# A graph layer and a routed FFN on one core: phase 3 begins with the pair of blocks that phase 2 ends with, two FFN chunks go ahead, batch norms take a power on GpSimd

## The chip, the core and the metric

The kernel runs on one core of one Trainium2 chip, as one launch. The time is device microseconds (us) of the whole launch: the median of three runs is 2086.63 us (2084.45, 2086.63 and 2086.96).

A core has five engines that run side by side, each its own list of instructions in order: TensorE (PE in the profile, matrix products and transposes), VectorE (DVE), ScalarE (ACT), GpSimd (POOL) and SyncE (SP, which here only starts DMAs). They wait for each other by semaphores. SBUF is the on-chip memory of 128 partitions, PSUM the banks that matrix products write, HBM the memory outside. A scheduler orders the instructions of each engine from the order of the program text and estimated costs; `tc.keep_in_program_order` pins one.

## What is computed

```python
def ref(x, src, dst, edge_attr):            # x 10000 x 512, 5000 edges with 64 attributes
    xn = layernorm(x)
    msg = relu(xn[src] + edge_attr @ W_e + b_e)
    h = (1 + eps) * xn + segment_sum(msg, dst)
    h = silu(bn(h @ W1 + b1, g1, beta1))     # 512 -> 1024, bn: batch norm over all 10000 rows
    h = silu(bn(h @ W2 + b2, g2, beta2))     # 1024 -> 512
    x = x + h
    g = layernorm(x) in groups of 16 rows    # routed FFN: 16 experts in 4 sets
    perm = (logits == max over the 16 rows of a group),  logits = g @ controller + tie
    inner = relu(sum over rows of (g @ f1) * perm)
    return x + sum over expert, set of (inner @ f2) * perm
```

All is in float32. Both batch norms need the mean and variance of each feature over all 10000 rows, so nothing behind one can begin before the last row ahead of it is done.

## The kernel before

**Phase 1** gathers the 5000 source rows of x (40 tiles of 128, `xgs`), makes the messages and adds them into `agg` in HBM by indirect DMAs of GpSimd, each group of four after the one before.

**Phase 2** (loop L354-376) goes over ten pairs of blocks of 500 rows. A `Block` loads x and agg rows (`load`, L309-314, tiles `xt` and `at`), norms and adds them, and turns them feature-major into `hb`. `block_sums` (L110) makes five sums of quarters of `hb`, s1, s3 and s6 on GpSimd and s4 and s7 on VectorE; `strassen` (L125) makes the product with W1 from seven quarter products (named 1 to 7; in a profile by their PSUM banks w, v, y, z, x and so on) instead of eight. For each pair m runs over 4 slices of the output. The result h1 (two feature halves x two blocks x 500) gets its batch statistics by `bn_stats` and is stored to `h1s` in HBM.

**`batchnorm`** (L75) makes scale and shift of each feature: `bn_aggr` for each block of 128 features, then the root on ScalarE (`AF.Sqrt`), a reciprocal and three short operations on VectorE.

**Phase 3** (L379-400) makes the sums of W2's quarters (`weight_sums`, five VectorE instructions), and then for each of ten pairs loads `hb` (4 MB) from `h1s` in one DMA, applies batch norm and Silu in place on ScalarE (L388, 16 instructions), makes five block sums (L122, whole: kb is 4, so an instruction covers 4 x 500 or, where the profile shows 128x2000, all four slices) and runs `strassen` for m = 0 and 1. Only for the first pair the products come in the order `FIRST`, 2, 5, 4, 3, 1, 6, 7. The result goes to `h2s` in HBM in two stores a pair. `hb` has two buffers.

**The FFN** (L735 on) goes over 20 chunks of 512 rows (the last has 272). `load_y` reads four tiles `yt` of the chunk from `h2s`, `load_x` two tiles `x2` of x, `silu` applies batch norm 2 and Silu, `residual` transposes and adds, `norm` is the layer norm on GpSimd (its root as `ALU.pow` with the tile `power`), `flip` and `logits` and `choose` make the routing, `gather`, `inner`, `relu`, `outer`, `turn`, `split` and `scatter` the FFN. `step(a, b, d, e, nxt)` (L662-733) works on four chunks at once: a gets its residual, norm and routing, b its gather and first product, d its second product, e its way back; for `nxt`, the chunk after a, loads and Silu are issued.

```python
    chunks[0].load_y()
    chunks[0].load_x()
    chunks[0].silu()
    nc.sync.dma_start(out=f1_sb, in_=a["L0_ffn_f1"].rearrange("(k p) n -> p k n", p=P))
    ...
    for c in range(NC + 3):
        step(at(c), at(c - 1), at(c - 2), at(c - 3), at(c + 1))
```

The weights f1 (one DMA) and f2 (eight) are issued behind chunk 0's loads, on the same queue as all loads and stores (SP). The tiles `yt` have one buffer for each k, so a chunk's load waits for the residual of the chunk before.

Of the kernel before, what the change touches and what calls it, by code (L numbers as in the profile page):

```python
# [8 lines left out]
F32 = mybir.dt.float32  # L9
# [41 lines left out]
def gnn_ffn_kernel(ctx: ExitStack, tc: tile.TileContext, a: dict, out: bass.AP):  # L51
# [7 lines left out]
    h1s = tc.dram_tile([NP, P, MH, 2, TB], F32, name="h1s")  # L59
# [7 lines left out]
    power = const.tile([P, KH, 1], F32, name="power")  # L67
# [7 lines left out]
    def batchnorm(name, stats, blocks, g, beta):  # L75

        mv = const.tile([P, blocks, 2], F32, name=name + "_mv")
        sc = const.tile([P, blocks], F32, name=name + "_sc")
        sh = const.tile([P, blocks], F32, name=name + "_sh")
        for m in range(blocks):  # L80
            nc.vector.bn_aggr(out=mv[:, m, :], in_=stats[:, m, :, :].rearrange("p c s -> p (c s)"))
        nc.scalar.activation(sc, mv[:, :, 1], AF.Sqrt, bias=eps_t, scale=1.0)
        nc.vector.reciprocal(sc, sc)
        nc.vector.tensor_mul(sc, sc, g)
        nc.vector.tensor_mul(sh, mv[:, :, 0], sc)
        nc.vector.tensor_sub(sh, beta, sh)
        return sc, sh
# [22 lines left out]
    def block_sums(pool, name, hb, kb):  # L110

        def q(i, j):
            return hb[:, i * kb:(i + 1) * kb, j, :]

        r = {2: q(0, 0), 5: q(1, 1)}
        for n, eng, x0, x1, op in ((3, nc.gpsimd, q(0, 1), q(1, 1), ALU.subtract),
                                   (1, nc.gpsimd, q(0, 0), q(1, 1), ALU.add),
                                   (4, nc.vector, q(1, 0), q(0, 0), ALU.subtract),
                                   (6, nc.gpsimd, q(0, 0), q(0, 1), ALU.add),
                                   (7, nc.vector, q(1, 0), q(1, 1), ALU.add)):  # L120
            r[n] = pool.tile([P, kb, TB], F32, name=f"{name}_s{n}", bufs=1)
            eng.tensor_tensor(r[n], x0, x1, op)  # L122
        return r

    def strassen(ps, tmp, us, bs, kb, m, res, bias0, bias1, y, order=(3, 1, 2, 5, 4, 6, 7)):  # L125
# [4 lines left out]
        def product(n, bank, start):  # L130
            for k in range(kb):
                nc.tensor.matmul(bank, lhsT=us[n][:, k, m * P:(m + 1) * P], rhs=bs[n][:, k, :],  # L132
                                 start=start and k == 0, stop=k == kb - 1, skip_group_check=True)
# [29 lines left out]

    gnn = ExitStack()
    wa = gnn.enter_context(tc.tile_pool(name="wa", bufs=1))
    w2 = wa.tile([P, MH, H], F32, name="w2")
    wb = ExitStack()
# [4 lines left out]
    with tc.tile_pool(name="pa", bufs=2) as pa:  # L172
        with tc.tile_pool(name="pe1", bufs=1) as pe1, tc.tile_pool(name="pe", bufs=2) as pe, \
                tc.tile_pool(name="ps_e", bufs=2, space=PSUM) as ps_e:

            whole = E // TE

            def by_tile(name, past, dtype):
                flat = a[name][:whole * TE, :].rearrange("(t e) o -> t (e o)", e=TE)
                i = pe1.tile([NTE, TE], I32, name=name + "_i")  # L180
                nc.vector.memset(i, past)
                nc.sync.dma_start(out=i[:whole, :], in_=flat)
                nc.sync.dma_start(out=i[whole:NTE, :E - whole * TE], in_=a[name][whole * TE:E, :].rearrange("e o -> o e"))
                f = pe1.tile([NTE, TE], F32, name=name + "_r")
                nc.vector.tensor_copy(f, i)
                pt = ps_e.tile([TE, NTE], F32, name="row")
                nc.tensor.transpose(pt, f, ident[:NTE, :NTE])
                t = pe1.tile([TE, NTE], dtype, name=name + "_t")
                nc.vector.tensor_copy(t, pt)
                return t  # L190

            src_i = by_tile("src", 0, I32)
            dst_f = by_tile("dst", AGG_ROWS - 1, F32)
            eat = pe1.tile([ED + 1, EP], F32, name="eat")
            tc.keep_in_program_order(nc.vector.memset(eat[ED:ED + 1, :], 1.0))
            tc.keep_in_program_order(nc.vector.memset(eat[:ED, E:], 0.0))
            zero = pe1.tile([P, 1, H], F32, name="zero")
            nc.vector.memset(zero, 0.0)

            we = pe1.tile([ED + 1, H], F32, name="we")  # L200
            nc.sync.dma_start(out=we[:ED, :], in_=a["L0_gnn_W_e"])
            nc.sync.dma_start(out=we[ED:ED + 1, :], in_=a["L0_gnn_b_e"])

            nc.sync.dma_start(out=eat[:ED, :E], in_=a["edge_attr_64"])
            for r0 in range(0, AGG_ROWS, 8 * P):
                j = min(8, (AGG_ROWS - r0) // P)
                nc.sync.dma_start(out=agg[r0:r0 + j * P, :].rearrange("(p j) d -> p j d", j=j),  # L207
                                  in_=zero.to_broadcast([P, j, H]))


            before = pe1.tile([TE, EG, TE], F32, name="before")
            nc.gpsimd.memset(before, 1.0)
            nc.gpsimd.affine_select(out=before[:, EG - 1, :], in_=before[:, EG - 1, :], compare_op=ALU.is_gt, fill=0.0,
                                    base=0, pattern=[[-1, TE]], channel_multiplier=1)
            spare = pe1.tile([TE, EG], F32, name="spare")
            nc.gpsimd.iota(spare, pattern=[[TE, EG]], base=N, channel_multiplier=1,
                           allow_small_or_imprecise_dtypes=True)


            xgs = [w2[:, t, :] if t < MH else pe1.tile([TE, H], F32, name=f"xg{t}") for t in range(NTE)]  # L220
            for t in range(NTE):
                nc.gpsimd.indirect_dma_start(
                    out=xgs[t], out_offset=None, in_=x,
                    in_offset=bass.IndirectOffsetOnAxis(ap=src_i[:, t:t + 1], axis=0))

            last = []
            for g in range(NTE // EG):
                ts = slice(g * EG, (g + 1) * EG)

                row = ps_e.tile([TE, EG, TE], F32, name="row")  # L230
                for i in range(EG):
                    nc.tensor.transpose(row[:, i, :], dst_f[:, g * EG + i:g * EG + i + 1].to_broadcast([TE, TE]), ident)


                same = [pe.tile([TE, i + 1, TE], F32, name=f"same{i}") for i in range(EG)]
                count = pe.tile([TE, EG], F32, name="count")
                for i in range(EG):
                    r = row[:, :i + 1, :]
                    d = dst_f[:, g * EG + i:g * EG + i + 1]
                    nc.vector.tensor_scalar(same[i], r, d, None, op0=ALU.is_equal)  # L240
                    junk = pe.tile([TE, EG, TE], F32, name="junk", bufs=1)
                    nc.vector.scalar_tensor_tensor(junk[:, :i + 1, :], r, d, before[:, EG - 1 - i:, :],
                                                   op0=ALU.is_equal, op1=ALU.mult, accum_out=count[:, i:i + 1])


                rep = pe.tile([TE, EG], F32, name="rep")
                nc.vector.tensor_scalar(rep, count, 1.0, None, op0=ALU.min)
                away = pe.tile([TE, EG], F32, name="away")
                nc.vector.tensor_sub(away, spare, dst_f[:, ts])
                nc.vector.tensor_mul(away, away, rep)  # L250
                to_i = pe.tile([TE, EG], I32, name="to_i", bufs=NTE // EG)
                nc.vector.tensor_add(to_i, away, dst_f[:, ts])


                st = pe.tile([TE, EG, 6], F32, name="st")
                mv = pe.tile([TE, EG, 2], F32, name="mv")
                rs = pe.tile([TE, EG, 1], F32, name="rs")
                sh = pe.tile([TE, EG, 1], F32, name="sh")
                for i in range(EG):
                    nc.vector.bn_stats(out=st[:, i, :], in_=xgs[g * EG + i])  # L260
                    nc.vector.bn_aggr(out=mv[:, i, :], in_=st[:, i, :])
                nc.scalar.activation(rs, mv[:, :, 1:2], AF.Sqrt, bias=eps_t, scale=1.0)
                nc.vector.reciprocal(rs, rs)
                nc.vector.scalar_tensor_tensor(sh, mv[:, :, 0:1], -1.0, rs, op0=ALU.mult, op1=ALU.mult)
                for i in range(EG):
                    t = g * EG + i
                    xg = xgs[t]
                    pm = ps_e.tile([TE, H], F32, name="pm", bufs=3)
                    nc.tensor.matmul(pm, lhsT=eat[:, t * TE:(t + 1) * TE], rhs=we, start=True, stop=True)
# [542 lines left out]
```

## Time and profile before

| | |
|---|---|
| median of the runs | 2086.63 us |
| the profiled execution, its whole time | 2089.15 us |
| its span, first to last instruction | 2087.4 us |
| TensorE busy | 1862.4 us (89% of the span) |
| VectorE, ScalarE, GpSimd busy | 1134.8, 747.8, 600.9 us |
| last product of phase 2 ends | 754.87 us |
| last product of phase 3 ends | 1249.76 us |
| TensorE busy between 840 and 1240 us | 400.00 us |

One execution was profiled; all places in time below are us from the start of its span. Its page has the busy time of each engine, rows that cut the span into 40 slices of 52 us (a digit is tenths; the row PEclk is the TensorE clock that was granted, in tenths of full speed), and the chain of waits, which follows the work back from the last instruction. The trace behind it can be asked for one tile, one line of the kernel or one stretch of time. In a timeline a line has start, length, engine, line, operation, tiles (written<-read), shape and count, and in brackets the idle time ahead of it with what ended that idle time.

### The profile page before, as it was taken

What the parts mean: (1) busy time and instruction counts of PE and PEld (TensorE: products, weight loads), DVE (VectorE), ACT (ScalarE), POOL (GpSimd) and SP (SyncE); (2) the same over time, 40 slices, a digit from 0 to 9 for tenths busy, and PEclk for the clock granted to TensorE, in tenths of its full rate; (3) what the DMA queues carried; (4) which work ended last, traced back from release to release, by engine and by line L of the source; (5) the groups of instructions that cost most, each with busy time, mean ns of one, the idle gap of its engine ahead of it and who ended that gap; (6) DMA issues with size and microseconds to landing.
All of it is one profiled execution on the core that took longest, in us unless ns stands there. A gap on an engine that the chain in (4) does not pass through costs nothing.

```text
span 2087.4 us, 38115 instructions
## 1 busy us (share of the span) xinstructions
PE 1862.4 (89%) x16562; PEld 1042.8 (50%) x16562; DVE 1134.8 (54%) x1802; ACT 747.8 (36%) x1044; POOL 600.9 (29%) x536
## 2 busy tenths in 40 slices
PE   4885499999999969999999996899999999999884
PEld 2332244444444424444444444567666676666662
DVE  5743367777777755333333441365575565665655
ACT  1332233333333224332222203445454554545422
POOL 7145433333333205222232201112222222132311
PEclk8897699999999989999999996799999999999987
DMA  9976444444444152223323219122222222222101
GB/s 354 358 157 81 119 182 165 164 158 158 157 157 158 79 216 118 118 118 118 138 118 128 108 46 276 62 80 70 99 83 93 73 82 93 93 74 92 44 36 38
DMA packets 97069, 264.18 MB, mean 127 GB/s; under 512 B 7416, under 2 KB 8006, under 8 KB 95047
## 3 DMA queue, kind: packets, MB, share of 16 engines
q1 hardware_dynamic: 87942, 240.77, 31.3%
q0 software_dynamic: 8960, 20.98, 5.0%
q8 instruction: 130, 2.13, 0.4%
q14 instruction: 37, 0.30, 0.0%
HBM read 147.56 MB, written 114.16 MB: 125 GB/s over the span
## 4 chain that ended last, share of the span: by engine, by line
PE 62%; DVE 11%; DMA 9%; ACT 7%; POOL 5%; SPq 4%; issue 3%; POOLq 0%; DVEq 0%; ACTq 0%
PE z L132 9%; PE x L132 9%; PE pb L612 7%; PE pi L590 7%; PE pb L569 5%; PE v L132 5%; PE w L132 5%; PE pb L653 4%; SPq L207 3%; PE y L132 3%; PE pi L524 2%; DMA yt<-h2s 2%; DVE ln_st L323 2%; ACT xt L335 2%; ACT gs L575 2%
## 5 line engine op out<-in xcount | busy, mean ns | idle before, releaser
L122 POOL TENSOR_TENSOR h_s<-hb 128x1000 f32<-128x1000 f32 (+1 forms) x60 | 205.0, 3430 | 427.0 <-PE z L132 353.3
L132 PE MATMUL x<-h_s,w_u 128*128 128x500 f32 x640 | 288.2, 582 | 0.3 <-POOL h_s L122 0.3
L620 ACT COPY it<-pb 128x1024 f32<-128x1024 f32 x120 | 122.0, 1054 | 258.4 <-PE pb L612 258.4
L612 PE MATMUL pb<-f_sb,ib 64*64 64x256 f32 x2560 | 187.1, 389 | 10.1 <-DVE x L659 8.4
L132 PEld LDWEIGHTS x<-h_s,w_u 128*128 128x128 f32 x640 | 121.4, 190 | 147.5 <-issue 143.4
L626 DVE STREAM_TRANSPOSE it<-it 128x1024 f32<-128x1024 f32 x160 | 186.5, 1211 | 11.0 <-ACT it L620 11.0
L575 ACT COPY gs<-pb 128x1024 f32<-128x1024 f32 x152 | 153.0, 1064 | 104.1 <-PE pb L569 104.1
L590 PE MATMUL pi<-gs,f_sb 128*64 128x64 f32 x5120 | 178.8, 232 | 2.9 <-issue 2.9
L569 PE MATMUL pb<-bd,xl 32*128 32x128 f32 x2504 | 147.3, 307 | 36.0 <-ACT gs L575 29.1
L590 PEld LDWEIGHTS pi<-gs,f_sb 128*64 128x64 f32 x5120 | 167.5, 146 | 18.7 <-issue 12.4
L635 POOL TENSOR_TENSOR pv<-perm,odd_t 64x512 f32<-64x512 f32 (+1 forms) x80 | 99.7, 1247 | 233.6 <-PE pb L653 200.3
L132 PE MATMUL w<-hb,w_u 128*128 128x500 f32 x320 | 147.9, 596 | 19.7 <-ACT hb L388 19.7
L569 PEld LDWEIGHTS pb<-bd,xl 32*128 32x128 f32 x2504 | 118.2, 201 | 61.9 <-ACT gs L575 41.8
L132 PE MATMUL z<-h_s,w 128*128 128x500 f32 x320 | 147.1, 583 | 0.7 <-POOL h_s L122 0.7
L142 DVE SCALAR_TENSOR_TENSOR t<-w,s 128x500 f32<-128x500 f32 x60 | 40.6, 677 | 192.3 <-PE w L132 190.6
L132 PE MATMUL v<-hb,w_u 128*128 128x500 f32 x320 | 145.0, 586 | 0.0
L132 PE MATMUL z<-h_s,w_u 128*128 128x500 f32 x320 | 144.0, 582 | 0.3 <-POOL h_s L122 0.3
L612 PEld LDWEIGHTS pb<-f_sb,ib 64*64 64x64 f32 x2560 | 94.4, 133 | 86.8 <-issue 28.7
L137 ACT COPY s<-z 128x500 f32<-128x500 f32 x60 | 34.5, 575 | 278.2 <-PE z L132 220.1
L499 POOL TENSOR_SCALAR ln_rs<-ln_mv 128x4 f32<-128x4 f32 (+2 forms) x22 | 5.0, 225 | 421.0 <-DVE ln_mv L493 420.8
L388 ACT ACTIVATE hb<-hb,bn_sh,bn_sc 128x500 f32<-128x500 f32 x160 | 113.3, 794 | 0.0
L132 PEld LDWEIGHTS w<-hb,w_u 128*128 128x128 f32 x320 | 62.1, 195 | 95.1 <-issue 73.4
(135 smaller groups left out, 2692.4 us busy)
## 6 DMA issues: line engine op xcount, KB each, us to landing
h1s<-h SPq DMA_DIRECT2D x40, 1000.0 KB
hb<-h1s SPq DMA_DIRECT2D x10, 4000.0 KB
agg<-zero SPq DMA_DIRECT2D x10, 2048.0 KB
xt<-in_x_dram SPq DMA_DIRECT2D x20, 1000.0 KB
at<-agg SPq DMA_DIRECT2D x20, 1000.0 KB
h2s<-h SPq DMA_DIRECT2D x20, 1000.0 KB
x<-in_x_dram SPq DMA_DIRECT2D x39, 512.0 KB
out_dram<-x SPq DMA_DIRECT2D x39, 512.0 KB
```

The source lines that it names most:

```text
L122: eng.tensor_tensor(r[n], x0, x1, op)
L132: nc.tensor.matmul(bank, lhsT=us[n][:, k, m * P:(m + 1) * P], rhs=bs[n][:, k, :], start=start and k == 0, stop=k == kb - 1, skip_group_che ...
L207: nc.sync.dma_start(out=agg[r0:r0 + j * P, :].rearrange("(p j) d -> p j d", j=j), in_=zero.to_broadcast([P, j, H]))
L388: nc.scalar.activation(hb[:, m, t, :], hb[:, m, t, :], AF.Silu, bias=sh1[:, m:m + 1], scale=sc1[:, m:m + 1])
L569: nc.tensor.matmul(pg[r // 2][:, r % 2, j], lhsT=self.xl[j][s, k * P:(k + 1) * P], rhs=self.bd[s, j], start=True, stop=True)
L575: nc.scalar.copy(to[:, 8 * i:8 * i + 8], pg[i].rearrange("d r j e h -> d (r j) e h"))
L590: nc.tensor.matmul(self.pi[64 * q:64 * q + 64, m, :], lhsT=f1_sb[:, k, 2 * F * j:2 * F * (j + 1)], rhs=gs[:, :, j, :], start=(k == 0 and m ...
L612: nc.tensor.matmul(po[64 * dh:64 * dh + 64, q, t, :], lhsT=self.ib[s, 2 * b + t, :], rhs=f2_sb[s, 2 * b + t, HD * dh:HD * (dh + 1)], start ...
L620: nc.scalar.copy(dst, src)
L626: nc.vector.transpose(it, it)
L635: nc.gpsimd.tensor_tensor(self.pv[dh * ES:(dh + 1) * ES, :, o:o + n].rearrange("e v (q t) -> e v q t", q=q), self.perm[i * ES:(i + 1) * ES ...
L653: nc.tensor.matmul(pr[32 * r:32 * r + 32, dh, j % 2, :], lhsT=self.pv[s, v, tok], rhs=self.it[s, :, 2 * (4 * r + j) + v, :], start=(v == 0 ...
```

## The change

- **The last pair stays.** In phase 2's last pair each h1 slice is written into a tile of the pool of `xt` and `at` (`piece`) and isn't stored. Phase 3 takes the pairs in the order 9, 0, 1, ... 8; the first takes the kept pieces, the others load four pieces of 1 MB, alternately into tiles `hc` and into `xt`/`at` tiles. The pool `pa` therefore lives through phase 3.
- **Block sums by pieces.** As a pair now lies in four tiles, an instruction of phase 3's block sums covers one slice of 500: 12 on GpSimd and 8 on VectorE for a pair, where there were 3 and 2. The Silus of all pairs but the first cover two blocks (128x1000): 8 for a pair, where there were 16 of 128x500.
- **Batch norm by a power.** The root and reciprocal become an addition and a power on GpSimd; a Silu on one column (`warm`) follows phase 2 on ScalarE.
- **FFN ahead.** Chunks 0 and 1 both have loads and Silu ahead of f1 and f2; `step(0)` makes the residual and norm of chunk 1 too. A new pool `pre` holds the `yt` and `x2` of chunk 0: even chunks' `yt` are in it, odd ones' in `pf`. So `yt` has two buffers. With that pool there from the start, the scheduler issues chunk 0's `x2` load in phase 1 and its `yt` load in the middle of phase 3.

The core of the diff, with indentation changes left out:

```diff
     def batchnorm(name, stats, blocks, g, beta):
...
-        nc.scalar.activation(sc, mv[:, :, 1], AF.Sqrt, bias=eps_t, scale=1.0)
-        nc.vector.reciprocal(sc, sc)
+        nc.gpsimd.tensor_scalar(sc, mv[:, :, 1], EPS, None, op0=ALU.add)
+        nc.gpsimd.tensor_tensor(sc, sc, power[:, :blocks, 0], ALU.pow)
         nc.vector.tensor_mul(sc, sc, g)
...
-    def block_sums(pool, name, hb, kb):
+    def block_sums(pool, name, kb, q):
...
-            r[n] = pool.tile([P, kb, TB], F32, name=f"{name}_s{n}", bufs=1)
-            eng.tensor_tensor(r[n], x0, x1, op)
+            t = pool.tile([P, kb, TB], F32, name=f"{name}_s{n}", bufs=1)
+            r[n] = [t[:, k, :] for k in range(kb)]
+            for k0, k1 in [(0, kb)] if q(0, 0, 0, kb) is not None else [(k, k + 1) for k in range(kb)]:
+                eng.tensor_tensor(t[:, k0:k1], q(*x0, k0, k1), q(*x1, k0, k1), op)
...
+    pre = ctx.enter_context(tc.tile_pool(name="pre", bufs=1))
+    pre_y = [pre.tile([P, CH], F32, name=f"yt{k}") for k in range(KH)]
+    pre_x = [pre.tile([P, 2, H], F32, name=f"x2_{j}") for j in range(2)]
...
+        def piece(pool, name):
+            t = pool.tile([P, 4, H], F32, name=name)
+            return t.rearrange("p j d -> p (j d)")[:, :4 * TB].rearrange("p (r t n) -> p r t n", r=2, t=2)
...
-                    h1 = p2.tile([P, 2, 2, TB], F32, name="h1", bufs=2)
+                if more:
+                    h1 = p2.tile([P, 2, 2, TB], F32, name="h1", bufs=2)
+                else:
+                    h1 = piece(pa, ("xt", "at")[m % 2])
+                    pieces.append(h1)
...
-                    nc.sync.dma_start(out=h1s[i].rearrange("p (r m) t n -> p m r (t n)", r=2)[:, m],
-                                      in_=h1.rearrange("p r t n -> p r (t n)"))
+                if more:
+                    nc.sync.dma_start(out=h1s[i, m], in_=h1)
...
+    warm = const.tile([P, 1], F32, name="warm")
+    tc.keep_in_program_order(nc.scalar.activation(warm, eps_t, AF.Silu))
...
-        for i in range(NP):
-            hb = pb.tile([P, MH, 2, TB], F32, name="hb", bufs=2)
-            nc.sync.dma_start(out=hb, in_=h1s[i])
-            for half, t in ((0, 0), (1, 1), (1, 0), (0, 1)):
-                for m in range(4 * half, 4 * half + 4):
-                    nc.scalar.activation(hb[:, m, t, :], hb[:, m, t, :], AF.Silu, bias=sh1[:, m:m + 1],
-                                         scale=sc1[:, m:m + 1])
-            bs = block_sums(pb, "h", hb, 4)
+        for o, i in enumerate([NP - 1, *range(NP - 1)]):
+            if o > 0:
+                pieces = [pb.tile([P, 2, 2, TB], F32, name="hc", bufs=4) if o % 2 else
+                          piece(pa, ("xt", "at")[m % 2]) for m in range(4)]
+                for m in range(4):
+                    nc.sync.dma_start(out=pieces[m], in_=h1s[i, m])
+                for m in range(4):
+                    for r in range(2):
+                        h = pieces[m][:, r].rearrange("p t n -> p (t n)")
+                        nc.scalar.activation(h, h, AF.Silu, bias=sh1[:, 4 * r + m:4 * r + m + 1],
+                                             scale=sc1[:, 4 * r + m:4 * r + m + 1])
+            else:
+                for r, t in ((0, 0), (1, 1), (1, 0), (0, 1)):
+                    for m in range(4):
+                        h = pieces[m][:, r, t, :]
+                        nc.scalar.activation(h, h, AF.Silu, ...)
+            bs = block_sums(pb, "h", 4, lambda r, t, k0, k1: pieces[k0][:, r, t:t + 1, :] if k1 == k0 + 1 else None)
...
-                yt = pf.tile([P, CH], F32, name="yt", bufs=4)
+                yt = pf.tile([P, CH], F32, name="yt", bufs=4) if self.c % 2 else pre_y[k]
...
-                x2 = pf.tile([P, 2, H], F32, name="x2", bufs=8)
+                x2 = pf.tile([P, 2, H], F32, name="x2", bufs=6) if self.c % 4 else pre_x[j0 // 2]
...
-        put(a, Chunk.norm)
+        if a and a.c != 1:
+            a.norm()
+        if a and a.c == 0:
+            for j in range(len(nxt.tiles)):
+                nxt.residual(j)
+            nxt.norm()
         put(e, Chunk.split)
-        put(nxt, Chunk.load_y)
+        if nxt and nxt.c > 1:
+            nxt.load_y()
...
-    chunks[0].load_y()
-    chunks[0].load_x()
-    chunks[0].silu()
+    for c in range(2):
+        chunks[c].load_y()
+        chunks[c].load_x()
+        chunks[c].silu()
```

`load_x` and `silu` in `step` are guarded like `load_y`, and `res` like `norm`. In phase 1 four of the gathered tiles `xgs` lie in `pre_x` until they are scattered.

## The prediction

> **What bounds the kernel.** I read the page's slices first, for where TensorE isn't busy; then the chain of waits at those places; then the timeline, line and window views for durations.
>
> ```profile
> PE   4885499999999969999999996899999999999884
> PEclk8897699999999989999999996799999999999987
> DMA  9976444444444152223323219122222222222101
> ```
>
> A slice is 52.2 us. Past phase 1 TensorE is 90% busy or more but for slice 15 (783 to 835), slices 24 and 25 (1252 to 1357) and the tail. A window of phase 3, 840 to 1240, has 400.00 us of TensorE work in 400: VectorE (153), ScalarE (109) and GpSimd (106) have room. So outside the two seams only TensorE's own work counts, and the change takes none away. It can gain at the seams and lose by uncovering something.
>
> The chain over the first seam:
>
> ```profile
> 756.00 4.19 DMA h1s<-h
> ...
> 760.34 11.99 DMA hb<-h1s
> ...
> 773.72 11.23 ACT hb L388 x16
> ...
> 785.02 11.73 POOL h_s L122 x2
> ```
>
> Store of the last slice, its load back, all Silus, two sums: one after the other. TensorE idles 754.87 to 774.57 and then stutters to 796.79; its timeline:
>
> ```profile
> 774.57 6.61 PE L132 MATMUL w<-hb,w_u 128*128 128x500 f32 x8 [19.71 <-ACT hb L388]
> 781.01 3.52 PE L132 MATMUL v<-hb,w_u 128*128 128x500 f32 x8
> ```
>
> **First seam, step by step.** Store and load (16.3 us) and the table load behind them (1.28, made early by `warm`) leave the path. Next to be late is the batch norm: its statistics end at 757.85. Old: root to last subtraction, 759.03. New: wake of GpSimd 0.32 and an addition 0.23 (as in the FFN's norm), a gap of 0.08, the power, then 0.56 for mul, mul, sub. The only power row is this:
>
> ```profile
> 1268.52 1.03 POOL L500 TENSOR_TENSOR ln_rs<-ln_rs,power 128x4 f32<-128x4 f32 x1
> ```
>
> Here it has 8 elements a partition: 1.03 if its cost is fixed, 1.86 if it grows as the elements do above the 0.20 of a plain product of that size. I take 1.86: shift and scale at 760.9. The first product needs u2, a weight sum on VectorE behind the subtraction (a 1.15 us row): 762.1. It also needs only one Silu by then (0.72). TensorE starts at 762.2 (761.4 to 763.0) instead of 774.57: 12.4 gained.
>
> From there the order is 2, 5, 4, 3, 1, 6, 7. The idle gap shrinks from 19.7 to about 7.3 us. The cold row above (6.61 for eight, where the next eight take 3.52) came after 19.7 us; the Trainium skill, "TensorE: Matmul & The Clock Gate", Part 1, puts the fall to half clock after one idle window of about 3.4 us, which 7.3 exceeds too. With the clock kept, the seam would gain 3.1 more; the rule speaks against it and I follow the rule: w 762.2 to 768.8, v to 772.2, y (sum s4 by VectorE, early) to 775.7. Then s3 decides, on GpSimd, now in four pieces of 500. The rows for whole sums, columns min/median/max in ns:
>
> ```profile
> L122 POOL TENSOR_TENSOR h_s<-hb x60: 2295/3830/6447, 244.8 to 1199.6; 128x1000 f32<-128x1000 f32 x30, 128x2000 f32<-128x2000 f32 x30
> ...
> L122 DVE TENSOR_TENSOR h_s<-hb x40: 1178/1763/6466, 237.0 to 1203.5; 128x1000 f32<-128x1000 f32 x20, 128x2000 f32<-128x2000 f32 x20
> ```
>
> The shortest GpSimd sums are 2.295 for 1000 and 4.41 for 2000, so a line through them gives 1.24 for 500. ScalarE ends its sixteen half Silus at 761.0+11.4 = 772.4, and GpSimd, working s1 first (four pieces) and then s3 and s6 in turn as the slices come, ends s3 at 779.3. The same skill's page "SBUF — State Buffer", "Who interferes with whom", says that a VectorE instruction with two SBUF inputs and a GpSimd one that reads SBUF shut each other out for the whole instruction; the 6.45 beside 4.41 and VectorE's 6.47 beside its shortest 2.24 for the same shape agree. Three VectorE pieces (some 0.65, a line through 1.18 and 2.24) would then be added: 781.2. The last two products of z end 0.9 later, at 780.2 or 782.1, and x, z and x follow at 3.35 each: the seven products end at 790.3 to 792.1, before at 803.77; I take the middle. **First seam: -12.8** (-11.6 to -13.6). Of it 12.4 is the earlier start.
>
> **Later pairs of phase 3.** For a pair TensorE has 14 products of 3.35, 46.95 us. Beside them: GpSimd 12 pieces by 1.24 = 14.9 (whole: some 13), or 12 by 1.9 with the lock; VectorE 8 by 0.65; ScalarE 8 Silus of 1000 columns, not longer in sum than 16 of 0.72 (11.5). Four loads of 1 MB on SP instead of one of 4. The Silu of a pair two ahead sits ahead of ScalarE's copies for m = 1 and waits for a load whose tile must first come free; by the place of these I find it done about 4 us before the copy is wanted. Cost zero; with that cover gone, each us late costs one for each of nine pairs.
>
> **Second seam.** The chain before:
>
> ```profile
> 1250.56 4.21 DMA h2s<-h
> ...
> 1256.36 3.65 DMA yt<-h2s
> ...
> 1270.26 3.02 POOL xl L506 x4
> ...
> 1312.63 3.03 POOL xl L506 x4
> ```
>
> It shows chunk 0's norm, and 42 us later chunk 1's: with f1 and f2 on the same queue chunk 1 came late. TensorE idles once more for it, and the first gathers of chunk 1 are here:
>
> ```profile
> 1313.46 1.23 PE L514 MATMUL ps<-ident,xl 128*128 128x128 f32 x3 [6.26 <-POOL xl L506]
> ...
> 1325.48 0.49 PE L569 MATMUL pb<-bd,xl 32*128 32x128 f32 x4
> ```
>
> New: chunk 0's yt is loaded in phase 3, so its Silu starts when the shift is there: statistics at 1251.98, plus 0.32+0.23+0.08+1.03+0.56 = 1254.2, against 1259.13: 5.0 earlier. First gather 1277.6 for 1282.59; f1, issued behind chunk 1's loads at about 1255, lands near 1277 and is wanted only by the first inner product, near 1284. So 5.0 stays. In step 1 chunk 1's norm is already done and its routing follows inner(3) of chunk 0, at about 1300; choice 3.5 us, transposes 2.4: gather at 1306.4 for 1325.48, 19 earlier. In step 2 some of that goes back: the residual of chunk 2 is now placed among the products behind inner(1), and its VectorE and GpSimd chain (11 us from residual to norm, as at 1262.7 to 1273.3) is bare. I place the end of inner(1) at 1319 (1323 if the clock stays cold) and the gather of chunk 2 at 1344 to 1347, before 1360.07. **Second seam: -15** (-11 to -19).
>
> **Steady FFN.** A step takes 37.15 us, with small waits like this one in each:
>
> ```profile
> 1634.41 1.52 ACT L477 ACTIVATE yt<-yt,bn_sh,bn_sc 128x512 f32<-128x512 f32 x2 [1.43 <-DMA yt<-h2s]
> ...
> 1636.94 0.49 PE L569 MATMUL pb<-bd,xl 32*128 32x128 f32 x4 [0.73 <-ACT gs L575]
> ```
>
> ScalarE's Silu of the next chunk waits for a load that waits for the residual to free the tile; copies of the gather stand behind it, and TensorE behind them. The second set of yt tiles would end that, but in the changed order load and Silu are each for one chunk further on and sit at the same places: the load again waits for a residual of the same step. So no gain, except where there is no load left, in the last steps: **-1.4**, one step's three waits.
>
> **Phase 1.** Chunk 0's x2 load (1 MB) goes on SP before phase 2's first loads, about 135 us, while scatters run and DMA slices read 9, 9, 7, 6. A bound below is nothing (SP waits there for the scatters anyway), above 1 MB at 358 GB/s, 3 us: I take **+1**.
>
> Sum: -12.8-15-1.4+1 = -28.2. The profiled execution took 2089.15 (span 2087.4), so 2061.0; it is 2.5 above the median, which gives **2058.5** for the median of runs.
>
> **Rivals.** *A, the second yt tiles work after all* (chance 0.07). For: the load may land before its place on ScalarE comes. Against: its releaser is unchanged. It would give 16 steps by 1.1, and some 10 that steps with late loads (41.3, 38.7, 39.5, 41.0 for 37.15) lose: -56, 2031. *B, the second seam gives little* (0.12): chunk 2's residual and norm come bare, on a cold clock, beside f2's load. Then it is -6 and the total -19: 2068. *C, phase 3 is no longer bound by TensorE* (0.03): ScalarE waits in front of its copies for a 1 MB load that its tile's last reader released late. This decides if loads come over 4 us later than I place them; the seams' 28 are eaten at 3.1 us for each of nine pairs, and at 4 the time is 2095, slower. For it speaks that a tile is now freed in parts and loads are split; against, that DMA is 0.29 busy in phase 3's window. *The change not doing what it says* can be excluded for the seam: the order of the instructions has no store or load there.
>
> **Chances.** The forecast above has 0.78. The range, 2046 to 2069, takes in the bounds of both seams (ends -22 and -35, and 5 more at the lower end for a part of A, B at the upper): A and C are outside. About 0.2%, 4 us, can be told from no change. Faster 0.95, same 0.02, slower 0.03.
>
> **What would show it.** Right: first product of phase 3 7 us after phase 2's last, eight cold; seven products over within 36 us of phase 2's end (before 48.9); 46.95 us a pair; chunk 1's first gather about 29 us behind chunk 0's (before 42.9); steady steps of 37.15 us with the Silu still waiting for yt. Wrong: steps near 36 (A); a wait of z or x for ScalarE in phase 3 (C); a late chunk 2 (B); a power far from 1.0 to 1.9 us.

## The result

The changed kernel takes 2067.61 us (median of four runs, 2064.4 to 2074.38). Its ratio to before is 0.9921, interval 0.9896 to 0.9946, which on the 2086.63 us shown before is 2070.1 us: 1 us above the forecast range of 2046 to 2069. A second series of the same kernel, the control below, gave 0.9941 (0.9927 to 0.9955; 18 runs from 2063.5 to 2079.0, median 2070.06). The gain is 12 to 19 us, where 28 were forecast.

The rows of its page (40 slices, of 51.8 us here):

```profile
PE   7935499999999989999999996899989999999984
PEclk9967699999999999999999997899999999999987
DMA  9986444444444122322333209222222222222110
```

The dip of TensorE where phase 3 begins (the fifteenth digit, a 6 before) has shrunk to an 8. The dip where the FFN begins (the 25th and 26th digit, 6 and 8) is as it was, and the DMA row has its 9 there still. By stretches the profiled executions differ from the one of before so (us; in brackets what the stretch took before):

| stretch | forecast | profile | profile of the control |
|---|---|---|---|
| start to agg's first load (219.04 us before) | +1 | +2.2 | +2.2 |
| from there to phase 2's last product (535.83) | 0 | +0.8 | +0.7 |
| from there to the end of the first seven products (48.9) | -12.8 | -8.1 | -8.4 |
| the other 133 products of phase 3 (445.99) | 0 | 0.0 | 0.0 |
| phase 3's last product to chunk 2's first gather (110.3) | -15 | -6.7 | -7.5 |
| from there to the end (727.4) | -1.4 | -3.3 | -6.8 |

The first seam in the chain of waits:

```profile
761.30 1.68 POOL bn_sc L84
...
767.26 18.48 POOL h_s L123 x11
785.79 1.47 PE z L133 x2
787.26 4.68 PE x L133 x8
791.95 3.35 PE z L133 x8
```

Store and load are gone, TensorE starts 7.02 us after phase 2's last product (757.90). But eleven GpSimd pieces in a row hold z back to 787.3, and x then runs on a cold clock (4.68 for 3.35; the granted clock is 0.59 from 787.0 to 790.4). The timeline there, all engines:

```profile
774.67 3.32 POOL L123 TENSOR_TENSOR h_s<-xt 128x500 f32<-128x500 f32 x2
...
776.82 3.35 DVE L123 TENSOR_TENSOR h_s<-at 128x500 f32<-128x500 f32 x2
776.95 0.30 PEld L133 LDWEIGHTS y<-h_s,w 128*128 128x128 f32 x2 [1.34 <-DVE h_s L123]
```

Two pieces take 3.3 us on either engine, 1.65 each, at the same time. In later pairs a GpSimd piece takes 1.24 (median) and a VectorE piece 0.67.

The second seam in the chain:

```profile
1286.67 5.16 issue
...
1320.14 1.87 PE pb L645 x26
...
1326.47 1.28 DVE x L524 x2
...
1332.15 1.06 POOL ln_rs L533
1333.91 2.28 POOL xl L539 x3
...
1348.30 0.49 PE pb L602 x4
```

TensorE stands 5.16 us waiting for nothing that the profile shows (the view calls it "issue"; below I call it a wait without a releaser), while the DMA queues are full. Among chunk 1's gathers and inner products its clock is 0.52 for 7 us (columns: window, length, TensorE busy, clock, DMA share, GB/s):

```profile
1305.00:1312.00 7.00, 7.00 (x108) 0.52 0.01 2
```

Behind chunk 1's inner products (1320.14) comes chunk 2's residual on VectorE and its norm on GpSimd, with little under them, and then chunk 2's first gather.

A steady step has the wait it had before:

```profile
1544.56 0.81 ACT L510 ACTIVATE yt<-yt,bn_sh,bn_sc 128x512 f32<-128x512 f32 x1 [1.67 <-DMA yt<-h2s]
...
1547.09 0.81 ACT L510 ACTIVATE yt<-yt,bn_sh,bn_sc 128x512 f32<-128x512 f32 x1 [1.72 <-DMA yt<-h2s]
1547.81 2.05 ACT L608 COPY gs<-pb 128x1024 f32<-128x1024 f32 x2
...
1548.94 0.49 PE L602 MATMUL pb<-bd,xl 32*128 32x128 f32 x4 [2.82 <-ACT gs L608]
```

This is a step whose yt came late: the Silu waits twice for it, the gather's copy stands behind the Silu, and TensorE waits 2.82 us for the copy. Most steps take 37.15 us; this one took 40.6.

### The profile page after: what moved, and what is told of

It reads as the page before. It is cut to its first block, busy times and chain, and to the rows that moved or that the text cites. A ratio compares the mean times of both kernels' runs of the same rounds, so it can differ in the third digit from the quotient of the medians.

```text
span 2072.3 us, 38292 instructions
## 1 busy us (share of the span) xinstructions
PE 1858.1 (90%) x16562; PEld 1041.7 (50%) x16562; DVE 1145.5 (55%) x1860; ACT 726.4 (35%) x969; POOL 626.7 (30%) x630
## 4 chain that ended last, share of the span: by engine, by line
PE 66%; DVE 13%; DMA 7%; ACT 6%; POOL 5%; issue 3%; SPq 0%; DVEq 0%; POOLq 0%; ACTq 0%
PE x L133 9%; PE z L133 9%; PE pi L623 7%; PE pb L645 7%; PE v L133 5%; PE w L133 5%; PE pb L602 5%; PE pb L686 4%; PE pc L282 3%; PE y L133 3%; PE pi L557 2%; DVE ln_st L329 2%; DMA yt<-h2s 2%; ACT xt L341 2%; PE pt L133 2%
## 5 line engine op out<-in xcount | busy, mean ns | idle before, releaser
L602 PE MATMUL pb<-bd,xl 32*128 32x128 f32 x2504 | 143.6, 302 | 35.8 <-ACT gs L608 26.9
L123 POOL TENSOR_TENSOR h_s<-hc 128x500 f32<-128x500 f32 x60 | 77.0, 1319 | 148.7 <-PE z L133 148.7
L692 DVE TENSOR_TENSOR x<-pb,x 128x1024 f32<-128x1024 f32 (+1 forms) x40 | 48.2, 1208 | 101.9 <-PE pb L686 101.9
L686 PE MATMUL pb<-it,pv 64*32 64x256 f32 x2504 | 81.7, 395 | 20.8 <-DVE it L659 20.8
L348 PE MATMUL pt<-ident,xt 125*128 125x125 f32 x320 | 47.9, 288 | 56.6 <-DVE xt L342 47.8
L341 ACT ACTIVATE xt<-xt,ln_sh,ln_rs 125x512 f32<-125x512 f32 x80 | 59.6, 805 | 110.4 <-POOL ln_sh L336 110.4
```

Of the source, the lines that this page charges most:

```text
L123: eng.tensor_tensor(t[:, k0:k1], q(*x0, k0, k1), q(*x1, k0, k1), op)
L341: nc.scalar.activation(r, r, AF.Identity, bias=self.sh[:RT, j, :], scale=self.rs[:RT, j, :])
L602: nc.tensor.matmul(pg[r // 2][:, r % 2, j], lhsT=self.xl[j][s, k * P:(k + 1) * P], rhs=self.bd[s, j], start=True, stop=True)
L686: nc.tensor.matmul(pr[32 * r:32 * r + 32, dh, j % 2, :], lhsT=self.pv[s, v, tok], rhs=self.it[s, :, 2 * (4 * r + j) + v, :], start=(v == 0 ...
```

## The experiments

In the experiments "seven products" is the time from phase 2's last product to the end of the first seven of phase 3: 48.9 us before, 40.8 changed. A chunk's gather is counted from the start of its first product on TensorE, and a step from one chunk's first gather to the next one's. Ratios are to the kernel before, run beside each version.

**First pair's block sums on VectorE alone.**

```diff
-            bs = block_sums(pb, "h", 4, ...)
+            bs = block_sums(pb, "h", 4, ..., gp=nc.gpsimd if o else nc.vector)   # gp replaces nc.gpsimd in s3, s1, s6
```

> The changed kernel, with the block sums of phase 3's first pair all on VectorE (20 pieces; GpSimd has none of them). In the changed kernel each of the two engines takes 1.65 to 1.7 us for a piece there, and TensorE's first seven products end 40.7 us after phase 2's last. Theory (the two engines shut each other out, piece by piece; alone VectorE needs some 0.6 us): pieces of 0.6 to 0.65 us, all 20 done within 13 us of the weight sums' end, no stall of TensorE after the start, the seven products end 32 to 34 us after phase 2's last; total 7 us below the changed kernel, ratio to before near 0.989. Rival (a piece of 500 columns has a cost of its own of 1.65 us on either engine): 20 pieces take 33 us, the seven products end after 50 us or more; total 8 to 15 us above the changed kernel.

Measured: seven products 33.5 us, total 2062.87 us (ratio 0.9913, 0.9888 to 0.9938). The timeline:

```profile
770.02 0.67 DVE L123 TENSOR_TENSOR h_s<-xt 128x500 f32<-128x500 f32 x1
770.61 0.67 DVE L123 TENSOR_TENSOR h_s<-at 128x500 f32<-128x500 f32 x1
...
775.26 3.52 PE L133 MATMUL y<-h_s,w 128*128 128x500 f32 x8
778.62 3.52 PE L133 MATMUL z<-h_s,w 128*128 128x500 f32 x8
781.97 3.52 PE L133 MATMUL x<-h_s,w_u 128*128 128x500 f32 x8
```

VectorE starts a piece every 0.59 us; TensorE runs through, and the clock stays warm in x. One engine does alone in 11.9 us what took the two more than 18.5. The rival falls. The total is 4.7 us below the changed kernel's first series and 7.2 below the control, where the seam gives 7.3.

**Chunk 0's x2 loaded in phase 3.**

```diff
+            if o == 2:
+                for j in range(2):
+                    tc.keep_in_program_order(nc.sync.dma_start(out=pre_x[j], in_=...))
...
+                if self.c:
                     nc.sync.dma_start(out=x2[:real, :k, :], in_=self.rows(x, o, real, k))
```

> The changed kernel, with chunk 0's x2 (1 MB) loaded in the middle of phase 3 and not in phase 1. In the changed kernel the first load of agg starts at 221.2 us, before the change at 219.0. Theory (the load takes DMA time from the scatter beside it): the fourth group of scatters lands within 7 us (8.4 with the load, 6.7 before), agg's first load starts near 219.3, total 2 us less. Rival (scatters vary by themselves): the start stays anywhere from 219 to 222 with no tie to that group, total within 1 us.

In the timeline agg's first load starts here:

```profile
218.31 1.25 SPq L316 DMA_DIRECT2D at<-agg  x2
```

In the six profiles of kernels that load x2 in phase 1 this load starts from 221.2 to 222.3 us, in the six that load it in phase 3 from 216.4 to 218.9; in the two without it, 219.0 and 219.3. The fifth group of scatters starts 6.7 us after the fourth one's last issue, where it was 8.4. The load cost 2 us or more, not 1, and the rival falls: the two groups don't overlap. The total (2062.87, five runs from 2060.11 to 2073.05) is too wide to show it.

**The Silu pinned behind the gathers' copies.**

```diff
             nxt.load_x()
+            nxt.silu()
         put(d, Chunk.outer, 0)
...
         put(d, Chunk.outer, 3)
-        if nxt and nxt.c > 1:
-            nxt.silu()
...
-                nc.scalar.activation(self.yt[k][:, :self.n], ..., AF.Silu, ...)
+                act = nc.scalar.activation(self.yt[k][:, :self.n], ..., AF.Silu, ...)
+                if self.c > 1:
+                    tc.keep_in_program_order(act)
```

> The changed kernel, with each chunk's Silu (from chunk 2 on) pinned on ScalarE behind the four gathers' copies of the step instead of between them. In the changed kernel TensorE waits 24 us over the steps for gather copies, which stand behind a Silu that waits for yt. Theory (the order on ScalarE, not the number of yt tiles, keeps this wait): the waits for gather copies fall to 0.3 us a step, steps take 36.2 to 36.4 us for 37.15, slow yt loads (steps of 39 to 41) no longer show; total 17 to 24 us below the changed kernel, ratio to before 0.980 to 0.984. Rival (the load itself is late): the wait moves to the residual's transposes of the next step, steps stay at 37, total within 4 us. Second rival (ScalarE is full at the new place): the outer product's copies come late, steps 37 to 38.

Measured 2035.61 us, ratio 0.9782 (0.9757 to 0.9807). The timeline of a step:

```profile
1536.78 2.08 ACT L610 COPY gs<-pb 128x1024 f32<-128x1024 f32 x2 [1.12 <-PE pb L604]
...
1538.75 2.92 ACT L510 ACTIVATE yt<-yt,bn_sh,bn_sc 128x512 f32<-128x512 f32 x4
```

The Silus wait for nothing. All steps from chunk 2 to chunk 17 take 35.43 to 35.49 us. I had put the gain too small: 1.7 us a step over 15 steps is 25 us, and 10 go with the slow loads of the changed kernel's profile; I had counted the 24 us of waits that the view shows, and not the length of the steps.

**The same pin in the kernel before**, with one set of yt tiles:

> The kernel before, with nothing but the Silu pinned behind the four gathers' copies of a step (from chunk 2 on); yt has its one set of tiles. Theory (the order on ScalarE alone makes the wait, the second set of yt tiles isn't needed to be rid of it): steps of 35.4 to 35.6 us as in the changed kernel with the same pin, total 28 to 32 us below before, ratio 0.985 to 0.987. Rival (the pin works only because yt has two sets of tiles): steps stay at 37 or the wait moves to the residual's transposes, ratio above 0.995.

Measured 2046.48 us, ratio 0.9822 (0.9784 to 0.9859), steps of 35.44 to 35.49 us but for one of 35.74. Here too the Silus stand behind the last copy of a gather and wait for nothing:

```profile
1617.72 2.07 ACT L577 COPY gs<-pb 128x1024 f32<-128x1024 f32 x2 [1.12 <-PE pb L571]
...
1619.66 2.94 ACT L477 ACTIVATE yt<-yt,bn_sh,bn_sc 128x512 f32<-128x512 f32 x4
```

So the second set of tiles isn't needed. This change of order is worth 37 us here, twice the change under study or more; between the two kernels with the pin 8 us (by the ratios, whose intervals overlap) to 11 us (by the medians) are left. It was more than expected, since the slow yt loads cost 12 us in the profile of before and hide as well.

**f2 loaded behind chunk 2.**

```diff
-    for q in range(2): ... nc.sync.dma_start(out=f2_to[rows, :, t, :], ...)   # ahead of all steps
+        if nxt and nxt.c == 2:                                                   # in step 1, behind chunk 2's loads
+            load_f2()
```

> The changed kernel, with the eight f2 loads issued behind chunk 2's loads instead of ahead of them; by that the scheduler puts chunk 2's residual at the head of step 2 and not behind its inner products. In the changed kernel chunk 2's first gather comes 103.7 us after phase 3's last product and 45.9 us after chunk 1's. Theory (the place of the residual behind inner(1) leaves VectorE's and GpSimd's chain bare, some 10 us): the gather comes 34 to 37 us after chunk 1's and 92 to 95 us after the last product; total 8 to 11 us below the changed kernel. Rival (cold clock and waits for instructions beside full DMA queues make the loss): chunk 2's gather comes within 3 us of where it is, total within 3 us.

Chunk 2's first gather comes 38.5 us after chunk 1's (45.9 changed) and 97.2 after phase 3's last product (103.7): 6.5 us, where the theory had 9 to 12 and the rival 3 at most. So the bare chain is the larger part, and not all. Total 2064.26 us, ratio 0.9915 (0.9889 to 0.9941), which isn't told from the changed kernel. In TensorE's timeline the residual's transposes stand among the products of chunk 1's first gather:

```profile
1303.00 1.06 PE L523 MATMUL ps<-ident,yt 128*128 128x128 f32 x4
1303.99 0.80 PE L602 MATMUL pb<-bd,xl 32*128 32x128 f32 x4
1304.72 1.11 PE L523 MATMUL ps<-ident,yt 128*128 128x128 f32 x4
```

VectorE's and GpSimd's chain now lies under the inner products. What is left against 34 to 37 goes with a cold clock: 0.66 on the mean of the 17 us behind chunk 1's gather. Three waits without a releaser (0.77, 3.46, 1.68) lie ahead of that gather, and so in the 97.2.

**The control.** 

> The changed kernel as it is, a second profile. Theory: agg's first load at 221 to 222.5 us again (218.3 where x2 was loaded in phase 3), seven products of phase 3 end 40 to 41 us after phase 2's last product, chunk 2's first gather 45 to 46.5 us after chunk 1's; what differs from the first profile is in steps with slow yt loads. Total 2060 to 2070.

The seams came as expected: agg's load at 221.24, seven products 40.5 us, chunk 2's first gather 45.9 us behind chunk 1's again; the table has the rest. The total didn't: nine of the 18 runs lie above 2070 us, one at 2079.

**Both norms by root again.**

```diff
-        nc.gpsimd.tensor_scalar(sc, mv[:, :, 1], EPS, None, op0=ALU.add)
-        nc.gpsimd.tensor_tensor(sc, sc, power[:, :blocks, 0], ALU.pow)
+        nc.scalar.activation(sc, mv[:, :, 1], AF.Sqrt, bias=eps_t, scale=1.0)
+        nc.vector.reciprocal(sc, sc)
```

> The changed kernel, with the batch norms by root and reciprocal as before (ScalarE and VectorE) and without the early Silu column. In the changed kernel phase 3's first product starts 4.03 us after the end of bn1's statistics, of it 1.68 the power. Theory (the power costs more than it saves: root 0.30 and reciprocal, with the table load of Silu 1.28 beside VectorE's short operations): the start comes 2.4 to 3.0 us after the statistics' end, 1.0 to 1.6 us earlier than with the power. Rival (the table loads stand on the path: one of 1.28 for the root and one for the Silu): 4.3 us or more. Total within noise of the changed kernel; the seam's rows decide.

```profile
760.55 0.30 ACT L83 ACTIVATE bn_sc<-bn_mv,eps_t 128x8 f32<-128x8 f32 x1 [5.72 <-DVE bn_mv L82]
760.87 1.28 ACT L420 ACT_TABLE_LOAD   x1
760.88 0.20 DVE L84 RECIPROCAL bn_sc<-bn_sc 128x8 f32<-128x8 f32 x1 [0.37 <-ACT bn_sc L83]
...
763.06 2.01 PE L133 MATMUL w<-xt,w_u 128*128 128x500 f32 x2 [5.53 <-ACT xt L420]
```

The first product starts 2.5 us after the statistics' end (760.52) for 4.03, and 5.53 after phase 2's last for 7.02: at this seam the power costs 1.5 us. Only one table load is left on the path, and VectorE works beside it. At the second norm the root is 0.4 us faster as well (chunk 0's Silu starts 3.9 us after phase 3's last product for 4.3), but the first gather comes no earlier (28.6 us for 27.9). The total (2066.04, ratio 0.9926, 0.9899 to 0.9953) shows no difference.

**The four edits together.** 

> The changed kernel with all four edits so far: first pair's block sums on VectorE, chunk 0's x2 loaded in phase 3, Silu pinned, f2 loaded behind chunk 2. Theory (four separate losses, each in its own stretch of time, so they add): 31 (pin) + 7.3 (sums) + 3 (x2) + 7 (f2) = 48 us below the changed kernel, 2018 to 2022 us, ratio to before near 0.969. Rival (one loss covers another): above 2026.

Measured 2019.14 us, ratio 0.9701 (0.9667 to 0.9736); seven products 33.0 us, agg's load 218.53, chunk 2's gather 35.8 after chunk 1's, steps 35.46. They add.

**f2 by 64 partitions**, on top of the four edits.

```diff
-                for t in range(2): ... f2_to[64 * q + F * h:64 * q + F * (h + 1), :, t, :]
+                nc.sync.dma_start(out=f2_to[2 * F * q:2 * F * (q + 1), :, t, :], in_=f2[t, q])
```

> The changed kernel with the four edits, and f2 loaded in four DMAs of 64 partitions instead of eight of 32. With eight of 32 the DMA queues are full from 1250 to 1290 us at some 200 GB/s, and TensorE waits three times (2.85, 3.50 and 0.26 us) between the first gathers of chunks 0 and 1 for nothing that the profile shows, while an instruction packet is among the full queues. Theory (TensorE's program is fetched through the same full queues): f2 moves faster than 200 GB/s, the full stretch ends some 8 us earlier, these waits fall below 3 us in sum, chunk 1's first gather comes 28 to 29.5 us after chunk 0's (30.9); total 1 to 4 us below the four edits alone. Rival (they have another cause, or 64 partitions are no faster): the waits stay above 5 us in sum and the gather near 30.9.

A miss: f2 still moves at 182 to 224 GB/s by the DMA view, TensorE's waits without a releaser sum to 7.0 us between the two gathers, and the second comes 31.8 us after the first. The total, 2016.54 us (0.969, 0.9651 to 0.9729), isn't told from the four edits. The Trainium skill, "SBUF — State Buffer", Door 1, says that partitions 0 to 63 are reached by no more ports than 0 to 31 and gives 196 beside 189 GB/s; this run agrees, and I should have looked there first.

**And bn1 by root**, with the lines shown above for that norm alone.

> As the run beside it, and bn1 by root and reciprocal (bn2 keeps the power). Theory: phase 3's first product starts 5.5 us after phase 2's last for 7.0 us, as in the run with both norms by root; the seven products end 31 to 31.5 us after it for 32.9; total 1.5 us below the run beside it. Rival (the sums of W2's quarters on VectorE then decide the start): 6.2 us or more, total the same.

Seven products 31.2 us, start after 5.53, as expected. The total is 2011.76 us, ratio 0.9678 (0.9639 to 0.9717): 4.8 us below the run beside it where 1.5 were expected, with intervals that overlap; only 1.8 us of it is in this seam.

**Three eighths of f2 loaded in phase 3**, into a tile of the pool `pre`.

```diff
+            if o == 4:
+                load_f2(f2_early, 0, EB)          # EB = 3 of 8
...
-            load_f2()
+            load_f2(f2_late, EB, MF // 2)
```

> As the last run (four edits, f2 by 64 partitions, bn1 by root), and three eighths of f2 (1.5 MB) loaded in the middle of phase 3, where the DMA queues are 0.3 busy. In the last run the queues are full from 1234 to 1278 us, and TensorE waits 1.16 and 4.18 us for nothing that the profile shows between the first gathers of chunks 0 and 1. Theory (its program is fetched through the full queues): the full stretch ends some 7 us sooner, the 4.18 us wait, which comes late in it, falls below 1.5 us; chunk 1's first gather comes 26 to 28 us after chunk 0's (29.95), total 2 to 3 us below the last run. Rival (another cause): the waits stay above 5 us in sum and the gather near 30.

The waits without a releaser fell to 0.79 us, and chunk 1's gather comes 21.9 us after chunk 0's, where 26 to 28 was expected. But the scheduler had moved f1 into phase 3 as well (issued 6.6 us ahead of its last product; I take it that f1's place in SBUF came free earlier), and the queues were full only to 1274, so this run changes two things. Half of what was won was given back ahead of chunk 0's first gather, which comes 32.0 us after the last product for 27.9: chunk 1's yt stood behind three of chunk 2's. The total is 2010.7 us, ratio 0.9657 (0.9628 to 0.9687), 1 us below the last run where 2 to 3 were expected.

**Chunk 1's loads first.**

```diff
+                if self.c in (1, 2):
+                    tc.keep_in_program_order(dma)   # loads of yt and x2; f1's DMA written ahead of them
```

> As the last run, with chunk 1's loads of yt and x2 put ahead of chunk 2's on the queue and f1 ahead of both. In the last run f1 was loaded in phase 3 too, since its place in SBUF came free earlier; DMA queues were full only until 1274 us, the waits without a releaser fell from 5.9 to 0.8 us, but three of chunk 2's yt loads stood ahead of chunk 1's, and TensorE waited 6.6 us for chunk 1's Silu ahead of the first gather. Theory: that wait falls to 1 us or less, chunk 0's first gather comes 27 us after phase 3's last product (31.6 in the last run), chunk 1's 22 us later with the waits without a releaser still below 1.5 us; total 4 us below the last run, 2005 to 2008 us. Rival (waits for the program come back when the loads move): chunk 1's gather comes 26 us or more after chunk 0's, total within 1 us of the last run.

2008.74 us, ratio 0.9625 (0.9602 to 0.9648), the lowest median here. The waits without a releaser stay away (0.16 us), and chunk 1's gather comes 22.2 us behind chunk 0's. The rest is a miss: chunk 0's first gather comes 31.0 us after the last product, not 27, as TensorE still waits 4.5 us for chunk 1's Silu (3.0, 1.1, 0.4). Chunk 1's loads are issued 8.9 us after the last store to h2s, 4.4 in the run with bn1 by root, as f1 now runs beside that store. The 2 us below the last run are no more than noise.

## Why the prediction was right or wrong

- **The bound** was read right: outside the seams phase 3 has the same 446.0 us for 133 products, and no wait for a 1 MB load showed. Rival C didn't come.
- **Start of phase 3**: forecast 7.3 us after phase 2's last product, 7.02 measured; the power took 1.68 between the ends 1.03 and 1.86. I didn't ask what the old way would cost once its load was gone: 1.5 us less.
- **Clock gate**: the rule was right against "the clock is kept", but the eight products took 5.6 us, not 6.61 (the clock came back after six; 4.9 to 6.4 us over the profiles), so w and v were 1 us early.
- **Where the first seam failed**: "Three VectorE pieces (some 0.65 ...) would then be added ... I take the middle". The 1.24 for a piece alone was right. But VectorE has work for every one of GpSimd's pieces, so the eleven took 18.5 us in sum, not 11 times 1.24, 13.6; that sums on VectorE alone are faster is shown by the first experiment. The mutual exclusion that the skill's page "SBUF — State Buffer" states was the term to count for every piece, also for GpSimd's first two beside the W2 sums (1.98 and 2.23 us). Taken to the letter it is too much, though: 1.24 + 0.59 would be 1.83 us a piece, and 1.65 were measured. And the stutter brought a cold x, 1.3 us.
- **Where the second seam failed**: Silu's start and the first gather came as forecast (27.9 us after the last product; forecast 27.8), the gather of chunk 1 nearly (57.8; 56.6). What failed is "I place the end of inner(1) at 1319 (1323 if the clock stays cold)": it came 75.5 us after the last product, 69.2 forecast, 73.2 cold. From chunk 1's gather to there 17.7 us passed where the forecast has 12.6. The clock was 0.52 for 7.0 of them, which at a full clock would have been some 3.4 us less, and TensorE waited 1.15 us for a gather's copy. Chunk 2's gather followed after 28.2 us, where 25 to 28 were forecast with the residual bare. So the size of **rival B** came (-6.7 for its -6), to which I gave 0.12, but only one of its grounds is new, the cold clock: the bare residual was in my forecast too, and f2's load was over (DMA share 0.03 from chunk 1's gather to 1320). I took the warm clock, though the 5 us ahead of the cold ones have 1.83 us of TensorE work in them (1300 to 1305, chunk 1's choice of routing). No run here changes the clock alone.
- **Phases 1 and 2**: the x2 load was taken at +1 between 0 and 3; 2.2 came. The 0.8 in phase 2 have no cause found.
- **Steady FFN**: no gain from the second tiles, as argued from the order; rival A didn't come. The -3.3 and -6.8 at the end are mostly fewer slow yt loads than in the profile of before (-2.0 and -5.1 up to chunk 17): I took the 12 us of them in one execution for fixed.
- **Slips in the working**, on which nothing rests: the first dip of TensorE's row is at 731 to 783 us, not 783 to 835, where it is busy for 50.3 us of 52. The middle of the first seam's two ends is -12.6, and the upper ends of both seams give -23, not -22.

B's total was 2068 and 2067.6 was measured, in part by chance: the profiled execution, the slowest of the four, took 2074.4. In it the first seam and phases 1 and 2 lost 6.7 us more than B had, the second seam won 0.7 more, and the last row of the table 1.9 more. The control's profile, 4.7 us faster (2069.71), has 3.5 of these in the steady FFN; of the other executions there is no trace.

## What to carry to other kernels

Where a load ends late on an in-order engine, look at what stands behind its reader before adding buffers: an instruction that can wait for a DMA belongs behind the copies that free PSUM, and here that order was worth twice the change. Block sums split between VectorE and GpSimd on the path cost nearly the sum of both (1.65 us for a pair of pieces that take 1.24 and 0.59 alone), not the longer one; VectorE alone was faster. And a load "somewhere in the slack" is paid where the DMA beside it is on the path.

## Not expected of the hardware

TensorE waited 2.9 to 7.0 us in sum for nothing that the profile shows in every profile in which it worked beside full DMA queues between the first gathers of chunks 0 and 1 (1.3 and 5.16 us in the changed kernel), and 0.8 and 0.2 us in the two where the queues had emptied by 1274 us. A packet of the instruction queue is among the full ones in that stretch.

I had overlooked where these waits stand. Counted in TensorE's products, they come 128 apart in all twelve of the first profiles (some 256 instructions with the weight loads), and at the same two places of the program in every version of the changed kernel, near product 3104 and near 3232; in four of them also near 3360. In the two runs whose queues had emptied the first place still has its short wait (DMA share 1.05 there), and the second, with a share of 0.00, has none. This is what a program would show that is fetched in blocks of that size through the same queues. No run changes the fetch alone, so it stays an inference.

The slow yt loads, in three to five steps of an execution, have no cause found; behind the pin they cost next to nothing (one step of 35.74 us).
